# A smaller third block for each expert, and another opening of the state space block

## The chip, the cores and the metric

The kernel runs on one core of one Trainium2 chip. The metric is the device time of one execution in microseconds; of the kernel before it is the median of three runs, 2810.66 us (2804.3 to 2813.29). One more execution was profiled; its trace is what the lines below come from. Engines are called as the profile calls them: PE is TensorE (PEld its weight loads), DVE VectorE, ACT ScalarE, POOL GpSimd, SP the queue that issues most transfers.

## The reference

The reference is a chain of four blocks on x of shape (2, 1024, 512), each added to x after a layer norm without weights:

```python
x = x + attention(layernorm(x))       # 16 heads of 32, causal
x = x + experts(layernorm(x))         # 32 experts of 192, the best 8 of each token
x = x + state_space(layernorm(x))     # 16 heads, state 64, head 64, chunks of 64
x = x + ghost_ffn(layernorm(x))       # 1376 wide, weights looked up in a table of 16
```

The experts: logits are x @ gate_w.T; the best eight of each token get the softmax of their logits as weights, the others zero; an expert gives silu(x Wg) * (x Wu), times the weight, times Wd, and the sum over the experts is the output. The state space block projects x to an input, a gate, and for each head a step dt and vectors B and C; softplus of dt, negated, is the logarithm of the decay; its sums along a chunk give the decays between steps; the scanned output is gated by silu and projected back. All is in float32.

## The kernel before

Four stages follow each other in one program: attention with the routing of the tokens (0 to about 810 us in the trace), the experts (to about 1550), the state space block (to about 2320) and the feed-forward block.

**Slots.** The router gives each expert CAP slots in a table `rows` in DRAM. A row has 545 floats: the normalised token (512), its number, and its 32 weights. Tokens of the first batch fill an expert's slots from the front, those of the second from the back (`_Router.route`), so that an expert's front part can be computed while the second batch is still being routed. Tokens that find no slot are left for `_left_over`, a branch at the end of the experts. CAP is 640, five blocks of 128: a front part of two blocks (FRONTB) and a back part of three. Rows are written by indirect transfers on POOL (L296); all of `rows` is cleared beforehand by 160 transfers on SP.

**Experts.** `_Experts.order` lists 64 parts, a front or a back of an expert each. `part(p)` does, in this order: the first product of the gates (`gates(p, 0)`); `begin_turn(p + 1)`, which copies the weight and the number of each token of the next part on DVE (rw and tok, L1060 and L1061); the transposes of the next part's first two blocks (`turn_block`, L1070, copied out by ACT at L1071); `down(p - 1)`, the product of the part before with Wd (L1128 and L1133), scaled by rw on ACT (L1140) and added to the sums in DRAM by indirect transfers on POOL (L1142), one a block; then `gates(p, 1)`, the third block's transposes, `gates(p, 2)`, and the load of the rows of part p + 3 (`load_rows`, L1024, three buffers). A product of the gates has 128 weight columns and all tokens of the part as moving columns (L1080): 256 for a front, 384 for a back; three products of four chunks each a part. Its results go through ACT (silu, L1090, L1097) and DVE (L1093 hT, L1101 hU).

Between these steps the feed-forward block's weights are looked up on DVE (`_look_up`, L937 to L943, 27 pieces of 16 steps) and stored to DRAM by SP (L951), and the state space block's weights are fetched. In this stage the order of PE, DVE and ACT is the order in which the program is written; the order on POOL and SP is a planner's, from its own costs, and each queue runs in order.

**State space.** `prepare(st)` has four steps for each of eight stretches of 128 tokens: load and statistics; normalise and transpose (L1387); the product for dt (L1393), its way through DRAM to another layout (SP, L1400 and L1403) and softplus to la (ACT, DVE); the transposed la and its sums (la_ps L1423, cs_ps L1427 and L1428), stored as cs_rows, from which csb is loaded (L1484) for the decays dec (L1495). `features(st)` has 32 steps, one for a group of 128 columns of B, C, input and gate each (L1443, eight records of 256 columns), evacuated by ACT (L1460) and DVE (L1462) from two banks. `begin`, `weights` and `products` work on a chunk each. Before the loop over the stretches the kernel runs all of `prepare(0)` and `prepare(1)`, then all of `features(0)`; here a planner orders all engines, taking the order of the program as priority.

Of the kernel before, what the change touches and what calls it, by code (L numbers as in the profile page):

```python
# [12 lines left out]
AF = mybir.ActivationFunctionType  # L13
ALU = mybir.AluOpType
# [4 lines left out]
P = 128  # L19
B, T, D = 2, 1024, 512  # L20
# [18 lines left out]


CAPB = 5
CAP = CAPB * P
FRONTB = 2
BACK = CAP - FRONTB * P
ROW = D + 1 + E
# [62 lines left out]
class _Router:  # L108
# [8 lines left out]
    def __init__(self, tc, g, x_sb, a, pool, rows, acc, kept, left, ready):  # L117
# [18 lines left out]
        nc.gpsimd.iota(  # L136
            self.spare, pattern=[[P * TOPK, NBLK], [P, TOPK]], base=1 + E * CAP,
            channel_multiplier=1,
        )
        self.first = pool.tile([P, E], I32, tag="first", name="first")  # L140
        nc.gpsimd.iota(self.first, pattern=[[CAP, E]], base=1, channel_multiplier=0)
        self.last = pool.tile([P, E], I32, tag="last", name="last")
        nc.gpsimd.iota(self.last, pattern=[[CAP, E]], base=CAP, channel_multiplier=0)
        self.room = pool.tile([P, E], F32, tag="room", name="room")
# [16 lines left out]
    def second(self, bank):  # L161

        nc = self.tc.nc
        nc.vector.tensor_scalar(
            self.room, self.total(bank), -1.0, float(CAP), ALU.mult, ALU.add
        )
# [3 lines left out]
    def route(self, blocks, wk, row_of, bank, apart=False):  # L170
# [74 lines left out]
        def each(t):  # L245
            return t.unsqueeze(1).to_broadcast([P, n, E])
# [5 lines left out]
        else:  # L252
            nc.vector.scalar_tensor_tensor(valid, pp, float(CAP), chosen, ALU.is_lt, ALU.mult)
            nc.vector.tensor_tensor(key, pp, each(self.first), ALU.add)
# [68 lines left out]
def _after(tc, later, earlier, kind=mybir.DependencyClass.Sync):  # L323
    tc.add_manual_dep(
        later.ins, earlier.ins.name, mybir.DependencyInfo(kind, mybir.DependencyReason.DATA)
    )


def _attention(tc, g, x_sb, a, router, gates, load_gates, make_experts):


# [649 lines left out]
class _Experts:  # L981
# [25 lines left out]
    def expert(self, p):  # L1007
        return E - 1 - self.order[p][0]

    def blocks(self, p):  # L1010
        return (FRONTB, CAPB - FRONTB)[self.order[p][1]]

    def load_rows(self, p):
        if p >= len(self.order):
            return
        tc, e, n = self.tc, self.expert(p), self.blocks(p)
        back = self.order[p][1]
        xg = self.wk.tile([P, CAPB - FRONTB, ROW], F32, tag="xg", name="xg", bufs=3)[:, :n]

        needed = [  # L1020
            s for sent in self.router.sent[: 1 + back] for s in chain(*sent[: E - e])
        ]
        r = 1 + e * CAP + back * FRONTB * P
        got = tc.nc.sync.dma_start(  # L1024
            out=xg,
            in_=self.router.rows[r : r + n * P, :].rearrange("(n p) d -> p n d", p=P),
        )
        for s in needed:
            _after(tc, got, s)
        tc.declare_no_dep(  # L1030
            got.ins, group="sent", keep=[s.ins for s in needed],
            reason="the others bring no row of this part",
        )
        tc.add_to_no_dep_group("read", got.ins)
        self.xg[p] = xg

    def load_weights(self, n):
# [14 lines left out]
    def begin_turn(self, p):  # L1052
        if p >= len(self.order):
            return
        nc, n, xg = self.tc.nc, self.blocks(p), self.xg[p]
        most = CAPB - FRONTB
        xgT = self.wk.tile([P, NCC, most * P], F32, tag="xgT", name="xgT", bufs=2)
        tok = self.wk.tile([P, most], U32, tag="tok", name="tok", bufs=4)[:, :n]
        rw = self.wk.tile([P, most], F32, tag="rw", name="rw", bufs=4)[:, :n]
        nc.vector.tensor_copy(rw, xg[:, :, D + 1 + self.expert(p)])  # L1060
        nc.vector.tensor_copy(tok, xg[:, :, D])  # L1061
        self.turned[p] = xgT, tok, rw

    def turn_block(self, p, j):
        if p >= len(self.order) or j >= self.blocks(p):
            return
        nc, xg, xgT = self.tc.nc, self.xg[p], self.turned[p][0]
        pt = self.bank("t", [P, NCC, P], "xg_ps")
        for cc in range(NCC):
            nc.tensor.transpose(pt[:, cc, :], xg[:, j, cc * P : (cc + 1) * P], self.g["ident"])  # L1070
        nc.scalar.copy(xgT[:, :, j * P : (j + 1) * P], pt)  # L1071

    def gates(self, p, m):
        nc = self.tc.nc
        HB = P // 2
        cols = self.blocks(p) * P
        xgT, wgu = self.turned[p][0], self.loaded[self.expert(p)]
        pg = self.bank("g", [P, (CAPB - FRONTB) * P], "pg")[:, :cols]
        for cc in range(NCC):
            nc.tensor.matmul(  # L1080
                pg, lhsT=wgu[:, cc, m * P : (m + 1) * P], rhs=xgT[:, cc, :cols],
                start=cc == 0, stop=cc == NCC - 1,
            )
        most = (CAPB - FRONTB) * P
        if m == 0:
            hT = self.wk.tile([P, most], F32, tag="hT", name="hT", bufs=2)
            hU = self.wk.tile([P, FRONTB * P], F32, tag="hU", name="hU", bufs=2)
            s = self.wk.tile([P, most], F32, tag="s", name="s", bufs=3)
            self.made[p] = hT, hU, s
            self.first = nc.scalar.activation(s[:, :cols], pg, AF.Silu)  # L1090
        elif m == 1:
            hT, hU, s = self.made[p]
            nc.vector.tensor_tensor(hT[:, :cols], s[:, :cols], pg, ALU.mult)  # L1093
        else:
            hU = self.made[p][1]
            s = self.wk.tile([P, most], F32, tag="s", name="s", bufs=3)
            nc.scalar.activation(s[HB:, :cols], pg[:HB], AF.Silu)  # L1097


            for r, c0, c1 in ((0, 0, cols - P), (HB, P, cols)):  # L1100
                nc.vector.tensor_tensor(  # L1101
                    hU[r : r + HB, : c1 - c0], s[HB:, c0:c1], pg[HB:, c0:c1], ALU.mult
                )

    def down(self, p):

        if p < 0:
            return  # L1110
        nc = self.tc.nc
        HB, HD = P // 2, D // 2
        n = self.blocks(p)
        hT, hU, _ = self.made[p]
        wd, (_, tok, rw) = self.wds[self.order[p][0]], self.turned[p]

        pieces = []
        for j in (0, n - 1):
            o = self.bank("o", [P, D], "yo")
            pieces.append((j, o, slice(0, D), HB if j else 0))  # L1120
        sums = [(j, o) for j, o, _, _ in pieces]
        for j in range(1, n - 1):
            o = self.bank("m", [P, 2, D], "ym")
            for h in range(2):
                pieces.append((j, o[:, h, :HD], slice(h * HD, (h + 1) * HD), h * HB))
            sums.append((j, o[:, :, :HD]))
        for j, o, cols, _ in pieces:
            nc.tensor.matmul(  # L1128
                o, lhsT=hT[:, j * P : (j + 1) * P], rhs=wd[:, 0, cols], start=True, stop=False
            )  # L1130
        for j, o, cols, r in pieces:
            c = (j - 1 if r else j) * P
            nc.tensor.matmul(  # L1133
                o, lhsT=hU[r : r + HB, c : c + P], rhs=wd[r : r + HB, 1, cols],
                start=False, stop=True,
            )
        for j, o in sums:
            y = self.wk.tile([P, D], F32, tag="y", name="y", bufs=6)
            to = y.rearrange("p (h d) -> p h d", h=2) if len(o.shape) == 3 else y
            nc.scalar.activation(to, o, AF.Copy, scale=rw[:, j : j + 1])  # L1140
            to = self.turn % 2 if self.both else 1
            nc.gpsimd.indirect_dma_start(  # L1142
                out=self.router.acc[to][:, :],
                out_offset=bass.IndirectOffsetOnAxis(ap=tok[:, j : j + 1], axis=0),
                in_=y, in_offset=None, compute_op=ALU.add,
            )
            self.turn += 1

# [175 lines left out]
def _state_space(tc, g, a, w, acc, x3, then, big, last):  # L1324
# [6 lines left out]
    nc = tc.nc  # L1331
    HB = P // 2
    NROW = B * SCH
    with ExitStack() as ctx:
# [274 lines left out]
            for _ in range(n):  # L1609
                next(it, None)  # L1610

        for st in range(2):
            for _ in prepare(st):
                pass
        for _ in features(0):
            pass
        begun = begin(0)
        wgt = weights(0, begun[1])
        for st in range(NST):
# [6 lines left out]
            feats = features(st + 1) if st + 1 < NST else iter(())  # L1626
            out = project_out(st - 1) if st else iter(())
# [25 lines left out]
class _FeedForward:  # L1653
# [65 lines left out]
    def rest(self):  # L1719
        tc, g, nc = self.tc, self.g, self.tc.nc  # L1720
        with ExitStack() as ctx:
# [39 lines left out]
            for tt in range(NTT):  # L1761
# [5 lines left out]
                if tt + 1 < NTT:  # L1767
                    x = normalise(tt + 1)
            down(*pending)


@with_exitstack
def kernel(ctx: ExitStack, tc: tile.TileContext, a: dict, out: bass.AP):
# [95 lines left out]
    big = second.enter_context(tc.tile_pool(name="ss_big", bufs=2, reuse_waits="tile"))  # L1869
    last = _FeedForward(tc, g, x3, out, big)  # L1870
    _state_space(tc, g, a, w, acc, x3, last_weights, big, last)
    last.rest()
    second.close()
# [86 lines left out]
```

## Time and profile before

| | us |
|---|---|
| median of three runs | 2810.66 (2804.3 to 2813.29) |
| the profiled execution's own time | 2820.1 |
| its span, first to last instruction | 2818.4 |
| mean granted clock of TensorE | 0.982 |

Busy time by stretch of the profiled execution:

| stretch, us | what runs | PE | DVE | ACT | POOL | DMA share |
|---|---|---|---|---|---|---|
| 0 to 750 | attention, first routing | 700.88 | 376.62 | 288.13 | 211.32 | 0.38 |
| 750 to 1548 | last routing, experts | 772.44 | 586.10 | 266.34 | 334.58 | 0.89 |
| 1548 to 1580 | turn to the state space block | 13.55 | 12.82 | 7.12 | 4.66 | 0.58 |
| 1580 to 1650 | its first features | 63.28 | 22.66 | 28.09 | 2.77 | 0.10 |
| 1650 to 2320 | its loop | 658.72 | 346.83 | 281.65 | 75.03 | 0.17 |
| 2320 to 2818 | the rest of the feed-forward block | 494.20 | 80.39 | 61.80 | 7.33 | 0.07 |

How to read it: busy times of different engines lie beside each other. A stretch takes as long as the engine or the transfer that the others wait for; what another engine does in it costs nothing until it is late. The idle time in front of a group of instructions and its releaser, which the groups list, tell who was late. PEclk, or the granted clock, says which part of its full speed TensorE was allowed.

### The profile page before, as it was taken

The numbers are of one execution on the slowest core, as the hardware profiler recorded it, in microseconds if no ns is written. First come the engines' busy times: TensorE is split into PE (matmuls) and PEld (weight loads), VectorE is DVE, ScalarE is ACT, GpSimd is POOL, SyncE is SP. The second block draws the span as 40 slices with busy tenths as digits, with TensorE's granted clock in tenths as the row PEclk, the third lists the DMA queues.
The fourth block names the chain that finished last, engine by engine and source line by source line (L and its number), as shares of the span: only waits on it lengthen the run. The fifth ranks groups of instructions, "written<-read, shape, count | busy, mean of one in ns | idle before, by whom it ended". The sixth has DMA issues, their size and how long they took to land. (4 is left out here: it accounts for less than half of the span.)

```text
span 2818.4 us, 34644 instructions
## 1 busy us (share of the span) xinstructions
PE 2703.1 (96%) x11976; PEld 1624.1 (58%) x11976; DVE 1425.4 (51%) x3952; ACT 933.1 (33%) x1887; POOL 635.7 (23%) x787
## 2 busy tenths in 40 slices
PE   7999999998989899999999699999999999999999
PEld 3444444544465566666665587777777775444444
DVE  5555543655236788987775344554455453101100
ACT  1344432443323233333333333443444433101010
POOL 2222220433355634333333000110111010000000
PEclk9999999998989999999999799999999999999999
DMA  3376532212479999998886301111111140100000
GB/s 115 111 199 184 164 115 70 92 60 74 153 247 248 241 228 255 263 240 202 205 205 107 84 16 36 38 41 44 28 47 42 35 147 20 34 8 27 30 0 26
DMA packets 242793, 315.60 MB, mean 112 GB/s; under 512 B 60753, under 2 KB 129361, under 8 KB 241841
## 3 DMA queue, kind: packets, MB, share of 16 engines
q1 hardware_dynamic: 208320, 234.87, 28.0%
q0 software_dynamic: 33280, 77.68, 13.1%
q8 instruction: 98, 1.61, 0.2%
q10 hardware_dynamic: 1008, 0.73, 0.1%
q14 instruction: 87, 0.70, 0.1%
HBM read 160.17 MB, written 153.04 MB: 111 GB/s over the span
## 5 line engine op out<-in xcount | busy, mean ns | idle before, releaser
L1080 PE MATMUL pg<-xgT,wgu 128*128 128x256 f32 (+1 forms) x1536 | 447.2, 444 | 13.8 <-DVE hT L1093 12.7
L1080 PEld LDWEIGHTS pg<-xgT,wgu 128*128 128x128 f32 x1536 | 289.0, 194 | 161.1 <-issue 51.2
L1142 POOL DMA_INDIRECT acc<-y,tok x160 | 272.9, 1706 | 401.8 <-ACT y L1140 186.7
L943 DVE SCALAR_TENSOR_TENSOR acc<-hit,lut,acc 128x688 f32<-128x688 bf16 (+2 forms) x405 | 348.8, 861 | 14.4
L1443 PE MATMUL pf<-xT,win 128*128 128x256 f32 x1024 | 242.5, 385 | 5.5 <-ACT gate L1471 3.8
L653 ACT ACTIVATE pT<-st 128x512 f32<-128x512 f32 (+3 forms) x384 | 158.7, 497 | 180.6 <-PE st L640 158.0
L548 PE MATMUL sp<-ka,qa 64*128 64x512 f32 (+3 forms) x768 | 207.3, 511 | 8.1 <-DVE mx L569 4.0
L1443 PEld LDWEIGHTS pf<-xT,win 128*128 128x128 f32 x1024 | 187.0, 190 | 38.8 <-PE pf L1443 7.2
L640 PE MATMUL st<-qa,ka 64*128 64x512 f32 (+3 forms) x768 | 182.4, 512 | 2.3 <-issue 1.5
L569 DVE TENSOR_REDUCE mx<-sp 128x1 f32<-128x384 f32 (+3 forms) x352 | 167.3, 492 | 17.4 <-PE sp L548 10.7
L657 POOL TENSOR_SCALAR_AFFINE_SELECT pT<-pT 128x128 f32<-128x128 f32 x256 | 83.5, 338 | 390.2 <-ACT pT L653 378.3
L296 POOL DMA_INDIRECT rows<-row,idx x128 | 128.7, 1005 | 108.3 <-DVE chosen L282 43.6
L1750 PE MATMUL po<-wd,f_hT 128*128 128x512 f32 (+1 forms) x352 | 152.6, 592 | 0.0
L671 PE MATMUL y<-pT,v 128*64 128x512 f32 (+3 forms) x768 | 145.7, 512 | 4.6 <-ACT raw L608 3.1
L562 DVE CUSTOM_DVE_ANT_0 junk<-sp,cmask 128x128 f32<-128x128 f32 x256 | 73.3, 286 | 145.3 <-PE sp L548 135.4
L548 PEld LDWEIGHTS sp<-ka,qa 64*128 64x128 f32 x768 | 91.8, 187 | 93.5 <-issue 49.7
L1694 DVE TENSOR_TENSOR f_hT<-s,pu 128x512 f32<-128x512 f32 (+1 forms) x37 | 25.5, 688 | 232.8 <-PE pu L1688 232.8
L640 PEld LDWEIGHTS st<-qa,ka 64*128 64x128 f32 x768 | 102.3, 192 | 63.2 <-issue 36.9
L1515 POOL TENSOR_TENSOR cd<-ft_c,ec 128x256 f32<-128x256 f32 x56 | 40.8, 730 | 413.3 <-PE cb L1529 205.2
L1140 ACT ACTIVATE y<-yo,rw 128x512 f32<-128x512 f32 x128 | 81.2, 684 | 157.9 <-PE yo L1133 150.1
L1443 PE MATMUL pf<-xT,wc 128*128 128x256 f32 x512 | 125.0, 391 | 8.8 <-DVE ft_b L1462 5.2
L1688 PE MATMUL pg<-f_xT,wg 128*128 128x512 f32 (+1 forms) x296 | 133.4, 593 | 0.0
(213 smaller groups left out, 4034.3 us busy)
## 6 DMA issues: line engine op xcount, KB each, us to landing
rows<-blank SPq DMA_DIRECT2D x160, 272.5 KB
xg<-rows SPq DMA_DIRECT2D x32, 817.5 KB
xg<-rows SPq DMA_DIRECT2D x32, 545.0 KB
csb<-cs_rows SPq DMA_DIRECT2D x128, 128.0 KB
wgu<-in_wg_dram SPq DMA_DIRECT2D x32, 256.0 KB
wgu<-in_wu_dram SPq DMA_DIRECT2D x32, 256.0 KB
wd<-in_wd_dram SPq DMA_DIRECT2D x32, 256.0 KB
wd<-in_wd_dram SPq DMA_DIRECT2D x64, 128.0 KB
```

What stands on the lines that cost most here:

```text
L296: t = tc.nc.gpsimd.indirect_dma_start(out=self.rows[:, :], out_offset=bass.IndirectOffsetOnAxis(ap=idx[:, i, k : k + 1], axis=0), in_=xr[i ...
L548: nc.tensor.matmul(sp[hh][:, c0:c1], lhsT=q[half, pr, tb * P : (tb + 1) * P], rhs=k[half, pr, k0 * P : k1 * P], start=True, stop=True,)
L569: nc.vector.tensor_reduce(m[:, n : n + 1], sp[hh][:, c0:c1], AX.X, ALU.max)
L640: nc.tensor.matmul(st[:, c0:], lhsT=k[half, j // 2, kb * P : (kb + 1) * P], rhs=q[half, j // 2, qt * 512 + c0 : (qt + 1) * 512], start=Tru ...
L653: e = nc.scalar.activation(pT[:, c0:], st[:, c0:], AF.Exp)
L671: nc.tensor.matmul(y[j // 2][half, c0:], lhsT=v[:, kb, h // 2, h % 2 : h % 2 + 2, :].rearrange("p k d -> p (k d)"), rhs=ps[j][:, c0:], sta ...
L943: nc.vector.scalar_tensor_tensor(acc, hit, lut[:n, k : k + 1], acc, ALU.mult, ALU.add)
L1080: nc.tensor.matmul(pg, lhsT=wgu[:, cc, m * P : (m + 1) * P], rhs=xgT[:, cc, :cols], start=cc == 0, stop=cc == NCC - 1,)
L1142: nc.gpsimd.indirect_dma_start(out=self.router.acc[to][:, :], out_offset=bass.IndirectOffsetOnAxis(ap=tok[:, j : j + 1], axis=0), in_=y, i ...
L1443: nc.tensor.matmul(pf, lhsT=w[wn][:, cc, c0 : c0 + P], rhs=xT[st][:, cc], start=cc == 0, stop=cc == NCC - 1,)
L1688: nc.tensor.matmul(dst[:n, :], lhsT=w[:, cc, fc * P : fc * P + n], rhs=self.xT[tt][:, cc, :], start=cc == 0, stop=cc == NCC - 1,)
L1750: nc.tensor.matmul(po, lhsT=self.hT[tt][fc // 4][:n, fc % 4, j * P : (j + 1) * P], rhs=wd[:n, fc, :], start=fc == 0, stop=fc == NFC - 1,)
```

## The change

Two things change. First, an expert has 608 slots in place of 640: the third block of each back has 96 slots. Its rows are loaded by a transfer of their own, its transposes, copies, products and scatters take 96 tokens, and the gates of a back 352 columns. Second, the opening of the state space block no longer runs `prepare(0)`, `prepare(1)` and `features(0)` one after the other, but takes steps of the three in turn.

```diff
-CAP = CAPB * P
+LASTB = 96
+CAP = (CAPB - 1) * P + LASTB
...
+    def of_block(self, p, j):
+
+        return LASTB if j == CAPB - FRONTB - 1 else P
+
+    def columns(self, p):
+        return self.blocks(p) * P - self.order[p][1] * (P - LASTB)
...
-        got = tc.nc.sync.dma_start(
-            out=xg,
-            in_=self.router.rows[r : r + n * P, :].rearrange("(n p) d -> p n d", p=P),
-        )
...
+        pieces = [(
+            xg[:, : n - back],
+            rows[r : r + (n - back) * P, :].rearrange("(n p) d -> p n d", p=P),
+        )]
+        if back:
+            r += (n - 1) * P
+            pieces.append((xg[:LASTB, n - 1], rows[r : r + LASTB, :]))
+        for to, src in pieces:
+            got = tc.nc.sync.dma_start(out=to, in_=src)
...
-        nc.vector.tensor_copy(rw, xg[:, :, D + 1 + self.expert(p)])
-        nc.vector.tensor_copy(tok, xg[:, :, D])
+        c = D + 1 + self.expert(p)
+        for m, b in ((P, slice(0, 2)), (LASTB, slice(2, n))):
+            if n >= b.stop > b.start:
+                nc.vector.tensor_copy(rw[:m, b], xg[:m, b, c])
+                nc.vector.tensor_copy(tok[:m, b], xg[:m, b, D])
...
-            nc.tensor.transpose(pt[:, cc, :], xg[:, j, cc * P : (cc + 1) * P], self.g["ident"])
-        nc.scalar.copy(xgT[:, :, j * P : (j + 1) * P], pt)
+            nc.tensor.transpose(
+                pt[:, cc, :m], xg[:m, j, cc * P : (cc + 1) * P], self.g["ident"][:m, :m]
+            )
+        nc.scalar.copy(xgT[:, :, j * P : j * P + m], pt[:, :, :m])
...
-        cols = self.blocks(p) * P
+        cols = self.columns(p)
...
-                o, lhsT=hT[:, j * P : (j + 1) * P], rhs=wd[:, 0, cols], start=True, stop=False
+                o[:m], lhsT=hT[:, j * P : j * P + m], rhs=wd[:, 0, cols], start=True, stop=False
...
-                out_offset=bass.IndirectOffsetOnAxis(ap=tok[:, j : j + 1], axis=0),
-                in_=y, in_offset=None, compute_op=ALU.add,
+                out_offset=bass.IndirectOffsetOnAxis(ap=tok[:m, j : j + 1], axis=0),
+                in_=y[:m], in_offset=None, compute_op=ALU.add,
...
-        for st in range(2):
-            for _ in prepare(st):
-                pass
-        for _ in features(0):
-            pass
+
+        first, second, feats = prepare(0), prepare(1), features(0)
+        for of, n in ((first, 2), (feats, 6), (first, 1), (second, 1), (feats, 6), (first, 1),
+                      (second, 1), (feats, 4), (second, 1), (feats, 6), (second, 1), (feats, 11)):
+            for _ in range(n):
+                next(of, None)
```

More of the change, by code (lines that the diff above doesn't have):

```diff
@@ L1023, in load_rows @@
         r = 1 + e * CAP + back * FRONTB * P
-        got = tc.nc.sync.dma_start(
-            out=xg,
-            in_=self.router.rows[r : r + n * P, :].rearrange("(n p) d -> p n d", p=P),
-        )
[L1028 to L1034, printed above, removed]
+        rows = self.router.rows
+        pieces = [(
[7 more added lines that the diff above has]
+            got = tc.nc.sync.dma_start(out=to, in_=src)
+            for s in needed:
+                _after(tc, got, s)
+            tc.declare_no_dep(
+                got.ins, group="sent", keep=[s.ins for s in needed],
+                reason="the others bring no row of this part",
+            )
+            tc.add_to_no_dep_group("read", got.ins)
         self.xg[p] = xg
@@ L1068, in turn_block @@
         pt = self.bank("t", [P, NCC, P], "xg_ps")
+        m = self.of_block(p, j)
         for cc in range(NCC):
-            nc.tensor.transpose(pt[:, cc, :], xg[:, j, cc * P : (cc + 1) * P], self.g["ident"])
-        nc.scalar.copy(xgT[:, :, j * P : (j + 1) * P], pt)
+            nc.tensor.transpose(
+                pt[:, cc, :m], xg[:m, j, cc * P : (cc + 1) * P], self.g["ident"][:m, :m]
+            )
+        nc.scalar.copy(xgT[:, :, j * P : j * P + m], pt[:, :, :m])
     def gates(self, p, m):
@@ L1097, in gates @@
             nc.scalar.activation(s[HB:, :cols], pg[:HB], AF.Silu)
-            for r, c0, c1 in ((0, 0, cols - P), (HB, P, cols)):
+            for r, c0, c1 in ((0, 0, (self.blocks(p) - 1) * P), (HB, P, cols)):
                 nc.vector.tensor_tensor(
@@ L1127, in down @@
         for j, o, cols, _ in pieces:
+            m = self.of_block(p, j)
             nc.tensor.matmul(
-                o, lhsT=hT[:, j * P : (j + 1) * P], rhs=wd[:, 0, cols], start=True, stop=False
+                o[:m], lhsT=hT[:, j * P : j * P + m], rhs=wd[:, 0, cols], start=True, stop=False
             )
         for j, o, cols, r in pieces:
+            m = self.of_block(p, j)
             c = (j - 1 if r else j) * P
             nc.tensor.matmul(
-                o, lhsT=hU[r : r + HB, c : c + P], rhs=wd[r : r + HB, 1, cols],
+                o[:m], lhsT=hU[r : r + HB, c : c + m], rhs=wd[r : r + HB, 1, cols],
                 start=False, stop=True,
@@ L1139, in down @@
             to = y.rearrange("p (h d) -> p h d", h=2) if len(o.shape) == 3 else y
-            nc.scalar.activation(to, o, AF.Copy, scale=rw[:, j : j + 1])
+            m = self.of_block(p, j)
+            nc.scalar.activation(to[:m], o[:m], AF.Copy, scale=rw[:m, j : j + 1])
             to = self.turn % 2 if self.both else 1
```

## The prediction

> **What bounds the kernel now.** I read first the slices of the page, then stages (busy time by stretch), then the groups of the expert stage by shape, then TensorE's timeline. Columns of slices are 70.5 us each.
>
> ```profile
> PE   7999999998989899999999699999999999999999
> PEclk9999999998989999999999799999999999999999
> DMA  3376532212479999998886301111111140100000
> ```
>
> TensorE fills nearly every slice; the dip in column 23 is the turn from experts to state space. By stretch (PE, PEld, DVE, ACT, POOL busy us, then clock, DMA share, GB/s):
>
> ```profile
> 920.00:930.00 10.00, 5.36 (x11) 2.85 (x11) 9.31 (x20) 0.38 (x1) 7.16 (x6) 0.71 0.89 258
> 980.00:990.00 10.00, 8.57 (x25) 4.46 (x25) 9.66 (x19) 1.46 (x3) 4.14 (x3) 0.71 1.00 238
> 1018.00:1548.00 530.00, 530.00 (x2175) 336.88 (x2173) 424.76 (x903) 188.10 (x351) 201.53 (x119) 1.00 0.89 213
> 1200.00:1250.00 50.00, 50.00 (x210) 31.92 (x209) 44.87 (x87) 18.22 (x33) 18.33 (x11) 1.00 0.98 257
> ```
>
> From 1018 to 1548 us TensorE has no gap at full clock: it alone sets that stretch. Before, from 822 us on, about eight experts run with gaps (two of them shown). VectorE at 44.87 of 50 us and the DMA engines at 0.98 come next. By shape (busy us, mean ns, idle before):
>
> ```profile
> L1080 PE MATMUL pg<-xgT,wgu 128*128 128x384 f32 x768 | 266.6, 498 | 13.8 <-DVE hT L1093 12.7 <-DVE acc L943 1.1
> L1080 PE MATMUL pg<-xgT,wgu 128*128 128x256 f32 x719 | 173.1, 383 | 0.0
> L1070 PE MATMUL xg_ps<-ident,xg 128*128 128x128 f32 x616 | 83.7, 275 | 7.8 <-DMA xg<-rows 4.1 <-ACT xgT L1071 3.7
> L1060 DVE COPY rw<-xg 128x3 f32<-128x3 f32 x32 | 6.0, 187 | 4.7 <-DMA xg<-rows 4.6
> ```
>
> Each matmul of the gates leaves two records (12 products, 24 records a part). Means overlap in TensorE's pipeline; the pitch comes from the timeline (start, duration):
>
> ```profile
> 1034.66 7.15 PE L1080 MATMUL pg<-xgT,wgu 128*128 128x384 f32 x24
> 1057.01 7.15 PE L1080 MATMUL pg<-xgT,wgu 128*128 128x384 f32 x24
> ...
> 1582.87 0.25 PE L1423 MATMUL la_ps<-ident,la 32*128 32x32 f32 x1 [1.62 <-DVE la L1418]
> 1585.33 1.04 PE L1393 MATMUL dt_ps<-wdt,xT 128*128 128x16 f32 x8
> 1595.75 1.97 PE L1443 MATMUL pf<-xT,wc 128*128 128x256 f32 x8 [1.58 <-DVE ft_b L1462]
> 1601.09 1.19 PE L1443 MATMUL pf<-xT,wc 128*128 128x256 f32 x2 [1.79 <-DVE ft_b L1462]
> 1603.23 13.73 PE L1443 MATMUL pf<-xT,wc 128*128 128x256 f32 x54
> 1616.80 27.79 PE L1443 MATMUL pf<-xT,win 128*128 128x256 f32 x128
> ```
>
> An expert (front and back) takes 1057.01 - 1034.66 = 22.35 us. The start of the state space, 1566.8 to 1644.4 us, is TensorE with waits, and its clock sank:
>
> ```profile
> 1582.00:1586.00 4.00, 2.84 (x22) 2.39 (x22) 2.65 (x9) 2.14 (x7) 0.00 (x0) 1.00 0.03 6
> 1598.00:1602.00 4.00, 1.15 (x3) 0.63 (x3) 1.15 (x5) 3.49 (x8) 0.00 (x0) 0.77 0.29 76
> 1602.00:1606.00 4.00, 4.00 (x12) 2.86 (x12) 0.66 (x3) 0.00 (x0) 0.00 (x0) 0.50 0.02 4
> ```
>
> **Part 1, backs of 352 slots.** First, does the smaller room suffice? Routing the reference's own inputs puts at most 576 tokens on an expert (limit 608) and at most 294 of one batch (limit 352 for the second), so the branch for tokens left over stays untaken.
>
> Gates: 24 records a back stream 352 columns in place of 384. Pitch of 256 columns: 27.79/128 = 0.217 us; of 512 columns: the chain's piece at 2509.96 us has 112 records of po in 48.08 us, 0.429 us. That is 0.83 ns a column, 26.6 ns for 32, times 24 = 0.64 us an expert. In the gapless stretch of 530/22.35 = 23.7 experts all of it lies on the path: -15.2 us. For the eight earlier ones 8 x 0.64 = 5.1 us is the upper end; TensorE waits there for hT, behind VectorE's wait for scatters that still read tok (18.6 us in four waits), on a pace set by the sends and DMA, so part is waited away again, and a stall that moves can cost as much: -5.1 to +5.1, I take half the gain, -2.5.
>
> Transposes of the third block move 96 columns, but each still loads 128 columns of weights. The trace has a nearer row than any shorter transpose: the dt products with 16 columns at 1585.33 still go 0.11 us apart (8 until 1586.21), the pitch of the 128-column transposes. So 0; the other end is 4 x 26.6 ns x 32 = -3.4 us.
>
> The down products keep 512 moving columns, and their 96 weight columns load under the product before: 0. The other end: loads of 64 columns take 140 ns (those of pT), of 128 columns 190, so up to 25 ns less on four records a back, -3.2 in all. ScalarE (188 of 530 us) and POOL (202 of 530) narrow off the path: 0. Their cover is TensorE, and it is still there.
>
> VectorE gains two copies a back, 0.16 us each by the two-block rows (165 and 162 ns), and loses 0.03 us each on hT and the second hU (555 against 422 ns for 128 columns): +0.26 net. Per expert 44.87/50 x 22.35 = 20.06, then 20.3 of 21.7 us, 94%: still under TensorE, 0. If not, the second rival.
>
> SP issues a second load of 96 rows a back, 0.38 us each, and the weight loads and look-up stores queue behind it. In the built order a store of looked-up weights stands between the two pieces at two places. The rows are asked for at the end of part p and first read in part p+2, at least one part, some 11 us, later; TensorE waited for them once (4.1 us), VectorE once (4.6): 0. Bytes fall by 32 x 2180 B for rows and 64 KB for the scatter a back.
>
> **Part 2, features between steps.** The built order of all engines differs only up to the first bx_ps; after it, it is the same. Nothing is added: 32 feature groups, 16 transposes, 32 dt records stay. At full clock their pitches make 256 x 0.217 = 55.5, 16 x 0.11 = 1.8, 32 x 0.11 = 3.5, the small la and cs products 2: 62.8 us. The stage takes 77.6. Of the 14.8 over, 6.6 are waits (la 1.62 and 1.35, laT 0.28, ft_b 1.58 and 1.79), 5 the half clock up to 1576, the rest, 3, the second half clock from 1601 (54 records at 1603.23 until 1616.80, 13.57 where 11.7 would do, and 1 just before).
>
> Walking the new order with the same durations: the first dt splits, its second half behind two feature groups; five groups (8.7 us) then cover the chain from the dt copy to la, 10.4 us in this trace (1572.43 to 1582.82): la is still late, by about 1.7 us. Five more groups cover la to cs. SP's order has nine csb loads ahead of the second dt_rows; VectorE meets the first dec while its csb is in flight (6.3 us from the la copy here), with feature copies queued behind it, and TensorE runs two banks ahead: about 1.9 us. Then ten us of groups cover the second la: near 0.3. So 3.9 us of waits for 6.6, the first half clock kept, the second gone, since no two waits fall together: 62.8 + 5 + 3.9 = 71.7, that is -6. Ends: -9 (no wait) and -2 (waits as walked, with a loss of clock, and 1 more).
>
> The Trainium skill, TensorE: Matmul & The Clock Gate, section What's actually happening, lets the clock fall to half only after an idle window of about 3.4 us. This trace differs: no wait near 1600 us exceeded 1.79 us, yet 0.50 was granted at 1602. By the page this loss need not return (-6); by the rows a crowd of waits brings it (-3).
>
> **Sum.** -15.2 - 2.5 - 6 = -23.7. The profiled execution took 2820.1 us (span 2818.4 and 1.7 around it), 9.4 above the median of the runs, 2810.66; -23.7 gives 2796.4 for such an execution, and 2787 for the median, my forecast.
>
> **Rivals.** (a) VectorE binds while look-ups are 688 wide (1018 to 1250, 10.4 experts): its 2.3 us of idle an expert are waits at fixed places of its order, and could stay. Then those experts lose 0.64 and pay 0.26: -23.7 + 9.4 = -14.3, 2796. For: 44.87 of 50. Against: the waits before hT are for TensorE and shrink with it. 0.08.
>
> (b) Part 2 gives nothing: waits move and the clock sinks again. -17.7, 2793. For: the planner had already put features between these steps. Against: 32 records stood ahead of la, now 56. 0.10.
>
> (c) The early stalls, 21.6 us of TensorE's time from 820 to 1000, grow by half, since sends and scatters keep their pace: +10.8 in place of -2.5, -10.4, 2800. 0.04.
>
> (d) The DMA engines, 0.98 at 1200, bind from 1050 to 1250 (nine experts) by the split load. A small transfer's round trip, from dt_rows issued at 1572.46 to the dependent load at 1574.07, is 1.6 us; fully exposed: 9 x 1.6 = 14.4, and the 0.64 x 9 lost: -23.7 + 20.2, 2807. Against: bytes fall, and TensorE never waited there. 0.06. The Trainium skill, DMA: Bandwidth & Descriptors, section Bandwidth, wants transfers of 1 MiB, with 64 KB at 138 GB/s against 341; the split goes against that rule, and no row here shows the two sizes alone.
>
> (e) Slower: the 96-row piece comes late, and VectorE's copies and the third transposes wait for it, gates behind them. It decides from 23.7/32 = 0.74 us a back. At the 1.2 us by which SP's longest issue of rows (1.54) exceeds the usual (0.38): +38.4, 2825. For: one queue in order, and a store in between. Against: 11 us of slack. 0.06.
>
> **How the numbers follow.** The forecast has the remaining 0.66. Its own range, 2775 to 2799, takes the ends of the terms (-35.9 and -12.1). The whole range adds (a) to (c), and the spread of the runs, some 4 us to either side: 2772 to 2804, leaving out (d) and (e). No change means within 0.3%, 8.4 us, about what a measurement here tells. Faster: 0.66 + 0.08 + 0.10 + 0.02 = 0.86; same: (d) and half of (c), 0.08; slower: (e), 0.06.
>
> **What will show it.** Right: the period near 21.7 us with no gap of TensorE after some 1010 us; gates of 352 columns 0.30 us apart, third transposes still 0.11; 1566.8 to bx_ps near 72 us with one loss of clock. Wrong: waits of TensorE for hT with VectorE full (a), half clock again inside the features (b), PE or DVE waiting for xg (d, e), or a period unchanged, which would mean that columns do not set it.

## The result, and the profile after

The changed kernel took 2788.3 us (median of six runs, 2785.25 to 2792.22), the kernel before 2811.34 beside it (six runs): a ratio of 0.9921, 95% interval 0.991 to 0.9932, or -23.0 us. The forecast was 2787, from a sum of -23.7. In a later set of runs (e11) the ratio was 0.9926 (0.991 to 0.9943).

The profiled execution took 2791.15 us, span 2789.4, against 2820.1 before, a difference of 28.95. Part of it does not come from the change: the first gates start at 778.00 us in place of 785.85, and the change leaves TensorE's work up to there as it was (in the profile before, TensorE's clock was granted at 0.83 to 0.89 in stretches from 680 to 740 us; here at 0.94 and 0.89 from 660 to 700, and at 1.00 from 700 to 760). In the thirteen profiles of this case the first gates start anywhere from 778.0 to 796.0 us. So 7.85 of the 28.95 is chance. The rest, read at fixed points of TensorE's work:

| stretch | before, us | after, us | difference |
|---|---|---|---|
| first transposes of rows to last down product (experts) | 764.21 | 743.33 | -20.9 |
| of these, 23 periods | 23 x 22.35 | 23 x 21.63 | -16.6 |
| last down product to first xn_ps (turn) | 19.04 | 20.72 | +1.7 |
| first xn_ps to first bx_ps (opening) | 77.62 | 75.47 | -2.1 |
| from there to the end of TensorE's last product | 1169.78 | 1170.05 | +0.3 |

The slices of the page after the change (69.7 us each); the dip at the turn has moved one column to the left:

```profile
PE   7999999999998899999997899999999999999999
PEclk9999999999989999999999899999999999999999
DMA  3366532212479999998885211111111140000000
```

By stretch (PE, PEld, DVE, ACT, POOL busy us, then clock, DMA share, GB/s):

```profile
1000.00:1519.00 519.00, 517.59 (x2188) 337.18 (x2189) 431.17 (x958) 185.81 (x352) 206.37 (x121) 1.00 0.89 214
1200.00:1250.00 50.00, 50.00 (x216) 32.86 (x216) 47.13 (x97) 17.97 (x34) 19.37 (x12) 1.00 0.96 233
```

TensorE still fills the stretch at full clock, with one wait of 1.41 us at 1168.24. VectorE went from 44.87 to 47.13 of 50 us: 47.13/50 x 21.63 = 20.4 us an expert, 94%.

Groups by shape between 1000 and 1510 us (busy us, mean ns, idle before):

```profile
L1100 PE MATMUL pg<-xgT,wgu 128*128 128x352 f32 x576 | 180.8, 464 | 1.4 <-DVE hT L1113 1.4
L1100 PE MATMUL pg<-xgT,wgu 128*128 128x256 f32 x552 | 133.5, 385 | 0.0
L1088 PE MATMUL xg_ps<-ident,xg 96*128 96x96 f32 x96 | 11.9, 246 | 0.0
```

TensorE's timeline around one back (start, duration):

```profile
1021.39 6.73 PE L1100 MATMUL pg<-xgT,wgu 128*128 128x352 f32 x24
1027.95 1.04 PE L1088 MATMUL xg_ps<-ident,xg 128*128 128x128 f32 x8
1028.83 1.88 PE L1149 MATMUL yo<-wd,hT 128*128 128x512 f32 x4
...
1031.50 1.12 PE L1155 MATMUL yo<-wd,hU 64*128 64x512 f32 x4
1032.45 0.61 PE L1155 MATMUL ym<-wd,hU 64*128 64x256 f32 x4
1032.99 1.99 PE L1100 MATMUL pg<-xgT,wgu 128*128 128x256 f32 x8
1034.82 0.49 PE L1088 MATMUL xg_ps<-ident,xg 96*128 96x96 f32 x4
1035.15 4.29 PE L1100 MATMUL pg<-xgT,wgu 128*128 128x256 f32 x16
...
1043.02 3.23 PE L1100 MATMUL pg<-xgT,wgu 128*128 128x352 f32 x10
```

The same places in the kernel before:

```profile
1481.71 7.15 PE L1080 MATMUL pg<-xgT,wgu 128*128 128x384 f32 x24
1488.70 1.04 PE L1070 MATMUL xg_ps<-ident,xg 128*128 128x128 f32 x8
...
1495.57 0.60 PE L1070 MATMUL xg_ps<-ident,xg 128*128 128x128 f32 x4
1496.01 4.47 PE L1080 MATMUL pg<-xgT,wgu 128*128 128x256 f32 x16
```

The period is 1043.02 - 1021.39 = 21.63 us. The row labelled 352 x24 holds the last sixteen records of a back and the first eight of the next front: to its successor it takes 6.56 us (1027.95 - 1021.39), before it was 6.99 (1481.71 to 1488.70). That is 0.43/16 = 27 ns a record. The four third transposes take 1035.15 - 1034.82 = 0.33 us; before they took 0.44 (1495.57 to 1496.01).

The opening on the same timeline:

```profile
1560.09 0.25 PE L1446 MATMUL la_ps<-ident,la 32*128 32x32 f32 x1 [1.25 <-DVE la L1441]
...
1577.81 1.97 PE L1466 MATMUL pf<-xT,wc 128*128 128x256 f32 x8 [1.67 <-DVE ft_c L1485]
1579.61 1.85 PE L1416 MATMUL dt_ps<-wdt,xT 128*128 128x16 f32 x16
1581.31 7.15 PE L1466 MATMUL pf<-xT,win 128*128 128x256 f32 x32
1591.61 5.38 PE L1466 MATMUL pf<-xT,win 128*128 128x256 f32 x16 [3.14 <-DVE ft_x L1485]
1596.92 0.24 PE L1446 MATMUL la_ps<-ident,la 32*128 32x32 f32 x1
```

The wait for la and the wait at ft_c (dec in front of the copies, its csb still in flight) are those of the walk, 1.25 and 1.67 us. The second la is not late at all. But a wait of 3.14 us for ft_x stands before it, and the sixteen records behind it take 5.38 us, where sixteen at full clock take 3.69 (1618.56 in the timeline of the second experiment, below). All engines between the second dt and that wait:

```profile
1581.50 0.19 DVE L1421 COPY dt<-dt_ps 128x32 f32<-128x32 f32 x1 [1.24 <-PE dt_ps L1416]
1581.72 0.36 SPq L1423 DMA_DIRECT2D dt_rows<-dt  x1
...
1585.40 0.32 SPq L1426 DMA_DIRECT2D d<-dt_rows  x1
...
1588.05 0.22 DVE L1431 TENSOR_SCALAR neg<-d 32x128 f32<-32x128 f32 x1 [1.79 <-DMA d<-dt_rows]
...
1589.14 1.28 ACT L1434 ACT_TABLE_LOAD   x1
...
1590.78 0.36 DVE L1441 TENSOR_TENSOR la<-neg,d 32x128 f32<-32x128 f32 x1 [1.33 <-ACT d L1434]
1591.17 0.62 DVE L1485 COPY ft_x<-pf 64x128 f32<-64x128 f32 x2
```

VectorE's neg waits for d, ScalarE's exponential for VectorE, then a table load of 1.28 us, then la: VectorE's copies of ft_x stand behind all of it, and TensorE has no free bank until 1591.61.

### The profile page after: what moved, and what is told of

Its sections match the earlier page's. It is cut to its first block, busy times and chain, and to the rows that moved or that the text cites. A ratio compares the mean times of both kernels' runs of the same rounds, so it can differ in the third digit from the quotient of the medians.

```text
span 2789.4 us, 34767 instructions
## 1 busy us (share of the span) xinstructions
PE 2674.8 (96%) x11976; PEld 1616.1 (58%) x11976; DVE 1428.9 (51%) x4016; ACT 925.9 (33%) x1886; POOL 635.4 (23%) x787
## 5 line engine op out<-in xcount | busy, mean ns | idle before, releaser
L1100 PE MATMUL pg<-xgT,wgu 128*128 128x256 f32 (+1 forms) x1536 | 429.0, 432 | 20.1 <-DVE hT L1113 18.1
L1163 ACT ACTIVATE y<-yo,rw 128x512 f32<-128x512 f32 (+1 forms) x128 | 80.8, 682 | 160.3 <-PE yo L1155 160.3
L1712 PE MATMUL pu<-f_xT,wu 128*128 128x512 f32 (+1 forms) x296 | 133.2, 592 | 0.0
```

The lines of the kernel that those rows point to most:

```text
L1100: nc.tensor.matmul(pg, lhsT=wgu[:, cc, m * P : (m + 1) * P], rhs=xgT[:, cc, :cols], start=cc == 0, stop=cc == NCC - 1,)
L1712: nc.tensor.matmul(dst[:n, :], lhsT=w[:, cc, fc * P : fc * P + n], rhs=self.xT[tt][:, cc, :], start=cc == 0, stop=cc == NCC - 1,)
```

## The experiments

Every set of runs had the kernel before beside it on the same chip; its median was 2811 to 2830 us from set to set, so ratios are compared, and single profiles by stretches.

**Each part alone (e1, e2).** The slots without the new opening:

```diff
-        first, second, feats = prepare(0), prepare(1), features(0)
-        for of, n in ((first, 2), (feats, 6), ...
+        for st in range(2):
+            for _ in prepare(st):
+                pass
+        for _ in features(0):
+            pass
```

> The slots alone, the opening of the state space as before. My theory, with the sizes that the trace of the changed kernel gave: an expert of 21.63 us in place of 22.35 for 23 experts is -16.6, the eight early ones -4.7 there (from -7.85 at the first gates to -12.55 at the first gapless back), so about -21 us, 2790, a ratio of 0.9925; the period stays 21.63 us and the opening stays near 77.6. By the terms as predicted (transposes nothing, early -2.5): -17.7, 2793.5, 0.9937. If the slots alone make the whole gain and the opening nothing: -23, 2788, 0.9918.

Measured: 0.9932 (0.9911 to 0.9953), -19 us. The period is 21.63, the experts take 751.2 us (with two stalls of TensorE, 7.38 us until 809.9 and 6.82 until 851.7, in which VectorE and ScalarE stand for most of the time too), the opening 78.86. The interval holds all three ratios that were expected; it is the period and the opening that agree with the first theory.

The new opening in the kernel with 640 slots:

> The opening alone, 640 slots as before. As the prediction's walk has it: -6 us, 2805, a ratio of 0.9979, 1566.8 to bx_ps down from 77.6 to about 71.7. As the trace of the changed kernel has it: -2.1 us, 2809, 0.9993, with waits near 1.3 (la), 1.7 (ft_c) and 3.1 (ft_x) and a fall of the clock behind the last. Its rival: nothing or a loss, the wait before the first xn_ps 1.7 us longer as in that trace (20.1 for 18.5): 1.0000.

Measured: 0.998 (0.9968 to 0.9992), -5.6 us. The period stays 22.35 and the experts 764.5, the opening takes 72.89 in place of 77.62. So the two parts add up, 19 + 6 for 23, and the opening gives more than the one profile of the changed kernel showed. What differs is the wait for ft_x:

```profile
1609.27 7.15 PE L1443 MATMUL pf<-xT,win 128*128 128x256 f32 x32
1618.56 3.69 PE L1443 MATMUL pf<-xT,win 128*128 128x256 f32 x16 [2.14 <-DVE ft_x L1462]
```

2.14 us here, and the records behind it run at full clock. In the changed kernel the clock was granted at 0.50 from 1592.30 to 1595.71, which loses half of 3.41 us; with 0.9 us more of waits (6.2 for 5.3) that makes the 2.6 us between the two openings.

**The third transposes (e4).** They go back to 128 rows and columns; the 32 rows more are read by a third load of each back:

```diff
-                pt[:, cc, :m], xg[:m, j, cc * P : (cc + 1) * P], self.g["ident"][:m, :m]
+                pt[:, cc, :], xg[:, j, cc * P : (cc + 1) * P], self.g["ident"]
...
+            pieces.append((xg[LASTB:, n - 1], rows[r : r + P - LASTB, :]))
```

> Only the transposes of the third block go back to 128 rows and 128 columns, all else as changed; the 32 rows more that they read come by a third load of each back. If the transposes' cost goes by their moving columns: four of them 0.44 us a back in place of 0.33, +0.11 x 32 = +3.4 at most, the period 21.74, 2791.5, a ratio of 0.9929. If it goes by the load of 128 weight columns, as the prediction took it: 0, 2788.3, 0.9918, with 0.33 us for the four in this run too. A third load a back that cost something on the path would show as waits for xg; by the slack of a part (11 us) it costs nothing.

```profile
1033.76 0.60 PE L1089 MATMUL xg_ps<-ident,xg 128*128 128x128 f32 x4
1034.20 4.26 PE L1101 MATMUL pg<-xgT,wgu 128*128 128x256 f32 x16
```

0.44 us for the four again, and a period of 21.71 in place of 21.63. The time, 0.9916 (0.9894 to 0.9939), cannot tell 3 us; the timeline does. So the 128 weight columns that each transpose loads, in both runs, do not set the price alone. Whether the moving columns or the rows of the weights do is not shown: both went from 96 to 128.

**More loads (e8).** Each block of rows gets a load of its own, five an expert:

```diff
+        for j in range(n):
+            m = self.of_block(p, j)
+            pieces.append((xg[:m, j], rows[r + j * P : r + j * P + m, :]))
```

> Every block of rows has its own load: five loads an expert in place of three, same bytes. If a split load cost anything on the path (rivals d and e of the prediction: 1.6 us a load fully exposed, or 1.2 a back), two more an expert would add 1.2 to 3.2 us an expert in the stretch where the DMA engines are at 0.98, nine to eleven experts, so +11 to +35, with waits for xg. If the slack of a part covers them, as I hold: 0 to the changed kernel, a ratio of 0.9918, and no wait for xg after 1010 us.

Measured: 0.9907 (0.9888 to 0.9927), the period 21.63, and no wait of TensorE over 0.3 us between 985 us and the end of the experts. A split load costs nothing on the path here: rivals (d) and (e) fall.

**Another 32 columns (e3, e5, e9).** Blocks of 64, `LASTB = 64`:

> Another 32 columns off each back (576 slots, third block of 64), the new opening kept. Theory that columns of TensorE set the period: again 24 x 26.6 ns + 4 x 26.6 ns = 0.75 us an expert by the price of a column, 0.72 by the step just seen: 20.9 us a period, -17 us in 23 experts and up to -5 in the early ones, so about 2768 and a ratio of 0.984 to before; third transposes of 64 columns 0.055 us apart. Rival that VectorE binds: it has 20.4 us of work an expert while the look-ups are 688 wide (1018 to 1250 us), 20.9 leaves it 0.5; if its waits at fixed places stay, those 11 experts gain nothing: -17 + 8 = -9, 2779, 0.9885, with waits of TensorE for hT between 1018 and 1250.

Measured: 0.9996 (0.9982 to 1.0009): the whole gain is gone, and neither theory foresaw that. TensorE has no gap after 990 us, so VectorE isn't it; the period itself is 22.76 us:

```profile
1066.92 2.03 PE L1149 MATMUL yo<-wd,hT 128*128 128x512 f32 x4
1068.88 1.13 PE L1149 MATMUL ym<-wd,hT 128*128 128x256 f32 x4
1069.94 2.12 PE L1155 MATMUL yo<-wd,hU 64*128 64x512 f32 x4
1071.99 0.70 PE L1155 MATMUL ym<-wd,hU 64*128 64x256 f32 x4
1072.62 1.99 PE L1100 MATMUL pg<-xgT,wgu 128*128 128x256 f32 x8
1074.55 0.46 PE L1088 MATMUL xg_ps<-ident,xg 64*128 64x64 f32 x4
1074.94 0.48 PE L1100 MATMUL pg<-xgT,wgu 128*128 128x256 f32 x1
```

The down products of a back take 1072.62 - 1066.92 = 5.70 us; in the changed kernel 1028.83 to 1032.99, 4.16. The largest piece is the row 64x512: these are the two half-row products of blocks 0 and 2, which in the changed kernel take 0.95 us for four records (1031.50 to 1032.45), here 2.05. There the first records of the two products start 7 ns apart; here each of the four records starts about 0.5 us after the one before. The gates kept their price (6.14 us from 1059.91 to 1066.05, 0.43 less than at 352 columns, sixteen records of 26.6 ns). So the theory was: where the third block's weights are 64 columns wide, half-row products no longer run side by side. To test it, the down products got 96 weight columns again, with 32 columns of filler:

```diff
+            if cols % P:
+                fill = DOWNB - LASTB
+                nc.scalar.copy(hT[:, cols : cols + fill], self.g["ident"][:, :fill])
+                nc.scalar.copy(hU[HB:, cols - P : cols - P + fill], self.g["ident"][HB:, :fill])
...
-            m = self.of_block(p, j)
+            m = max(DOWNB, self.of_block(p, j))
```

> 576 slots as in e3_last_64, but the down products of the third block keep 96 weight columns (32 of them filler, copied to hT and hU by ScalarE; their rows of the output are not read). Theory: e3 lost its columns' gain in the down products, where the two half-row products of 512 columns (64x128 and 64x64 weights) took 2.05 us in place of 0.94, and the others 0.1 to 0.2 more each; with 96 weight columns the pair runs side by side again, the period falls from 22.75 (e3) to 20.9 us, 0.72 below the changed kernel's 21.63, and the time by about 17 us against it: ratio near 0.9858. Rival, VectorE: it is at 20.4 us an expert until 1250 us, so the first eleven gapless experts stay near 21.6 with waits for hT, ratio near 0.989. Rival, the gates of 320 columns are themselves slow (0.256 us a record in e3 where 0.247 was expected): period 21.2.

Measured: 0.9886 (0.9867 to 0.9905). The period is 21.21, so 1.55 of e3's loss was the down products', just what they had grown by. It isn't 20.9: 0.33 us remain, and not in the gates of the back, whose sixteen records are at their price. They lie around the transposes, whose weights still have 64 rows and whose moving operand has 64 columns: eight front records before them take 1.92 us in place of 1.83, the four transposes 0.39 where two thirds of 0.33 were due (+0.17), and the records behind them 0.08 more than their columns say. So a block just above 64 should pay neither loss. `LASTB = 72`:

> 584 slots, third block of 72, everything else as changed: rows and columns of the third block's weights stay above 64. Theory that e3 and e5 lost their gain at blocks of 64 rows and columns (down products no longer side by side, and about 0.1 us more around each transposes' group of 64 rows): nothing of this happens at 72, and 24 columns less by 26.6 ns x 24/32 make 24 x 20 + 4 x 20 ns = 0.56 us an expert, a period of 21.07, -13 us in 23 experts to the changed kernel and up to -4 before: ratio 0.986 to 0.988. Rival, any block below 96 pays as e3 did (the loss goes by narrower weights, not by 64): a period of 22 or more, ratio near 1. Rival, VectorE: 20.4 us of work an expert in 21.07 until 1250 us, with waits for hT there: half of the gain, 0.990.

```profile
1093.41 6.41 PE L1100 MATMUL pg<-xgT,wgu 128*128 128x328 f32 x24
...
1103.21 1.12 PE L1155 MATMUL yo<-wd,hU 64*128 64x512 f32 x4
1104.13 0.63 PE L1155 MATMUL ym<-wd,hU 64*128 64x256 f32 x4
...
1106.52 0.42 PE L1088 MATMUL xg_ps<-ident,xg 72*128 72x72 f32 x4
1106.77 4.14 PE L1100 MATMUL pg<-xgT,wgu 128*128 128x256 f32 x16
...
1114.50 1.92 PE L1100 MATMUL pg<-xgT,wgu 128*128 128x328 f32 x6
```

The period is 21.09 (expected 21.07), four transposes take 0.25, the pair of half-row products 0.92. The time is 0.9874 (0.9858 to 0.989), 15 us below the changed kernel's 0.9926 in the same set. Of the widths that were run, 96 and 72 pay; at 64 the block loses more than it saves. VectorE, at the same place as above:

```profile
1200.00:1250.00 50.00, 50.00 (x218) 33.61 (x217) 47.94 (x96) 18.62 (x36) 21.73 (x12) 1.00 0.95 237
```

96%, and still TensorE has no gap: rival (a) would bind only beyond that.

**The early stalls (e6).** Eight buffers in place of four for what VectorE's tok copies fill:

```diff
-        tok = self.wk.tile([P, most], U32, tag="tok", name="tok", bufs=4)[:, :n]
-        rw = self.wk.tile([P, most], F32, tag="rw", name="rw", bufs=4)[:, :n]
+        tok = self.wk.tile([P, most], U32, tag="tok", name="tok", bufs=8)[:, :n]
+        rw = self.wk.tile([P, most], F32, tag="rw", name="rw", bufs=8)[:, :n]
```

> Eight buffers for tok and rw in place of four, all else as changed. Theory: TensorE's waits for hT between 880 and 1000 us (16.7 in four, in the changed kernel) come from VectorE's copies of tok, which wait for scatters that still read that buffer (21.9 us in five waits); with more buffers both go, and -10 to -17 us is left of the time to the changed kernel: a ratio of 0.986 to 0.988. Rival: the scatters are behind because of the sends before them, and the next to wait is ScalarE's y (six buffers) or the rows' loads; then the waits change their name and little is gained: 0.9918.

Waits from 820 to 1010 us, of the changed kernel (TensorE's, then VectorE's; us in total, times, longest):

```profile
PE pg L1100 <- DVE hT L1113: 16.7, 4, 5.7
...
DVE tok L1078 <- DMA acc<-y,tok: 32.1, 7, 6.4
```

and TensorE's and ScalarE's with eight buffers:

```profile
PE pg L1100 <- DVE hT L1113: 8.1, 2, 7.2
PE pg L1100 <- ACT xgT L1091: 6.9, 2, 5.5
...
ACT y L1163 <- DMA acc<-y,tok: 12.0, 5, 4.2
```

VectorE's wait for scatters is gone, and with it 15.8 of the 16.7 us (what is left under hT is one stall of 7.2 at 856 us, before the others, in which VectorE, ScalarE and TensorE stand together). Then ScalarE waits for the same scatters, for buffers of y, and holds xgT. The experts take 736.7 us, where the two profiles of the changed kernel have 743.3 and 745.7: 7 to 9 us, about half of what the waits measured. The time, 0.9898 (0.9881 to 0.9916), does not show it clear of noise: its interval overlaps that of the changed kernel (0.991 to 0.9932), and the profiled execution (2792.1 us) was some 8 us faster than the three others. By the profile, both theories were half right. More buffers for y were not run.

**The opening again (e7).** Two more places for features inside prepare: behind the load of d, and before la:

```diff
+            if apart:
+                yield
             neg = wk.tile([NROW, P], F32, tag="neg", name="neg", bufs=1)
...
+            if apart:
+                yield
             la = wk.tile([NROW, P], F32, tag="la", name="la", bufs=1)
```

> The opening again, with two more places between steps of the decays: two to six feature groups stand between the load of d and its first use, and one before la. Theory: TensorE's wait for ft_x (3.14 us in the changed kernel, 2.1 to 4.0 in its relatives) is VectorE's neg waiting for d with the feature copies behind it, and the wait for la (1.25) is the chain itself; both go, the second half clock with them, and ft_c's 1.6 stays: the opening 75.5 to about 69.5, -5 us to the changed kernel, a ratio of 0.990. Rival: the copies of ScalarE now wait behind its exponentials and table loads (1.28 us each), and the wait returns as ft_x or ft_b with another cause: within 1 us of the changed kernel, 0.9918.

Measured: 0.9915 (0.99 to 0.993), not to be told from the changed kernel. The opening takes 73.49 us, the clock falls once only, and the one wait of 3.14 has become four of 0.22 to 1.32 for ft_x. The first la still costs 1.25. The order that was built kept neg five copies of features behind the dt copy, and d's load was still in flight then (2.88 us of VectorE's wait): the gap has to be longer than the trip of d through DRAM, 6.5 us in the changed kernel and 7.5 here (1603.66 to 1611.21).

**All three (e10).** 72 rows, eight buffers of tok, and the opening with a wider gap:

> 584 slots as in e9_last_72, eight buffers for tok and rw as in e6_tok_8, and the opening of e7_opening_apart with la and the second half another group or three later. If the gains add: -13 to -17 by the slots, -6 by tok (experts 743.3 to 736.7 us there), -2 by the opening (75.5 to 73.5 there), so some -22 us to the changed kernel, a ratio of 0.984. If VectorE binds, which tok's buffers may relieve, or ScalarE's y waits for scatters in tok's place: -12, 0.988.

Measured: 0.9839 (0.9825 to 0.9853), 2775.17 us against 2820.22: faster than both kernels, about 24 us below the changed one (0.9926). Period 21.09, experts 727.6, opening 71.01.

**The changed kernel once more (e11)**, beside these two:

> The changed kernel itself beside the two others: 0.9918, its experts near 743 us and its opening near 75.5; how far these move between profiled executions bounds what the single traces tell.

0.9926; experts 745.65, opening 74.09, with a wait of 2.46 us for ft_x.

## Why the prediction was right

The forecast of -23.7 met -23.0, and the mechanism held: the columns of TensorE's products set the gapless stretch. By its terms:

- **Gates, -15.2.** Right. 27 ns a record in the trace of after, 0.43 us on sixteen records and the rest on eight; at 328 columns the same price again.
- **Transposes of the third block, 0.** Wrong, and mis-sized by the choice between two ends: they cost 0.33 us for four, -0.11 a back (the other end, -3.4 in all). The nearest row, dt products of 16 columns 0.11 us apart, was taken for a floor of all narrow products with 128 weight columns; 96 columns go 0.083 and 72 columns 0.063 us apart. The dt products were not as near as they looked: in the changed kernel's trace each of their weight loads takes 0.192 us at full clock, one of the transposes 0.141, with 128 rows and with 96. Why they stay at 0.11 wasn't tried; they have 128 rows, and in the transposes the rows fell together with the columns. With this term the period was due 0.64 + 0.11 = 0.75 lower; it fell by 0.72.
- **Down products, 0.** Right: 4.16 us a back, as before (1511.92 to 1516.09, 4.17). That they could grow was on no list; e3 showed that it needs 64 columns.
- **Eight early experts, -2.5.** Inside its ends. Experts less 23 periods: 250.2 before and 250.5 in e2; with 608 slots 245.8, 248.2 (e11), 248.2 (e7), 249.9 (e8), 252.2 (e4) and 253.7 (e1), a mean of -0.7 that single executions move by 4, so no gain is shown. The cause that was named for the waits, scatters that still read tok, was shown by e6.
- **VectorE, 0.** Right: 20.4 us an expert, predicted 20.3. The one wait of 1.41 us in the gapless stretch comes behind its tok copy, which had waited 2.27 us for a scatter at 1162.43. (The "second rival" to which the prediction points here is the one that it lists as (a).)
- **SP's second load, 0.** Right, by e8.
- **Opening, -6.** A term too large, within its ends in eight of nine profiles (71.9 to 75.5 us against 77.6; 76.7 in e8). The walk gave waits of 3.9 us; measured 4.8 to 7.0 in the nine profiles with this opening. The step that failed is "ten us of groups cover the second la": they do cover la, but the walk did not put VectorE's copies behind the chain of la in its queue, although it did so for dec two sentences before. Where the wait for ft_x stayed at 2.14 or 2.29 us (e2, e9), the clock held and the opening took 72.9 and 71.9 us, near the walk's 71.7; where it was 3.14 to 4.04 (the changed kernel, e4, e5, e8), the clock fell and it took 74.6 to 76.7. Between them lie e6 (2.50, held, 73.4), e3 and e11 (2.58 and 2.46, fell, 73.9 and 74.1).
- **The turn** was left out: 19.0 us in the one profile of before, 19.6 to 21.1 in all others, with 640 slots too (20.0 in e2).

Of the rivals, (a) is refuted by the trace and e9, (d) and (e) by e8. (b) came true in its mechanism and not in its price: waits moved, and the clock sank again inside the features in six of the nine profiles, but those openings still took 73.9 to 76.7 us where the old one takes 77.6 and 78.9 (e1), and e2 gains 5.6 us of time. (c) fell too: TensorE's waits in the experts were 23.8 us before and 24.9 after, not half as much again. That the two errors (3 us too little for transposes, 1 to 4 too much for the opening) cancelled is chance.

## What to carry to other kernels

Where TensorE had no gap, each column taken off the moving operand of a product was worth its pitch, and narrower transposes were cheaper too, at blocks of 96 and 72; at 64 rows or columns beside wider operands the gain was lost: look at the shapes that result, not only at the count. Put into an in-order queue's walk everything that stands behind a waiting instruction, each time, and not only at the place where it was first noticed. One profile's stretch can be off by several us (the same opening took 71.9 to 76.7): compare the same stretch in the profiles of relatives before sizing a term by it.

## What was not expected of the hardware

Two half-row products (64 rows on either half) of 512 columns ran side by side with weights of 128 and 128, 128 and 96, or 128 and 72 columns (0.92 to 0.96 us for four records) and one after the other with 128 and 64 (2.05 us). The other products of that group cost 0.09 to 0.24 us more each time as well. The Trainium skill, TensorEngine Tiling (Array Packing), section Tiling Modes, has 64 columns as a mode of the array with a drain at each change of mode; that fits these numbers, and that it is the cause is argued, not shown: the runs show only that the loss begins between 72 and 64.

The clock fell after waits of TensorE of less than 3.4 us. Around the wait for ft_x, which ends at 1591.61, the changed kernel was granted this:

```profile
1590.00:1595.00 5.00, 3.39 (x10) 2.79 (x11) 1.24 (x4) 1.77 (x6) 0.00 (x0) 0.73 0.02 5
```

It fell there after waits of 2.46 (e11), 2.58 (e3) and 3.14 to 4.04 us (the changed kernel, e4, e5, e8), to 0.50 to 0.71 in the five us from the wait's end, and held after 2.14 (e2), 2.29 (e9) and 2.50 us (e6). So the length of one wait does not decide it: 2.46 fell and 2.50 held, and in the old opening the same pair of waits, 1.6 us for la and 0.28 for laT, was followed by a fall in e1 and by none in the kernel before. Each fall inside an opening lasted 3.4 us or, in e8 and in the kernel before, twice that. The rule that the prediction took from the Trainium skill, TensorE: Matmul & The Clock Gate, an idle window of about 3.4 us, does not agree with the first of these.

Between 802 and 864 us, while the sends and the first experts share the DMA engines, nine of the eleven experiments' profiles have a stall of TensorE of 6.5 to 7.9 us, e1 two of them. In each, VectorE works for at most 1.4 us and ScalarE for at most 2.4. Three are put down to issue and to no semaphore (e1, e8, e11), the others to hT or xgT, which those two engines make. The profiles of before and after, e2 and e9 have no wait of more than 4.4 us there. Its cause is open. It is not the largest part of what single executions differ by: the first gates, before any of these stalls, start up to 18 us apart.
